# MLP gates in groups of four: modulation products in four row tiles, output turns as separate steps, gate and up weights in separate loads

## The chip, the cores and the metric

The kernel runs on one core of a Trainium2 chip. The metric is the device time of one execution in microseconds, as the median of several runs. The core's engines work side by side and each takes its instructions in the order written: TensorE (PE, matrix products, with the weight loads shown as PEld), VectorE (DVE), ScalarE (ACT), GpSimd (POOL) and SyncE (SP), which here issues nearly all DMA transfers. Data lie in SBUF, 128 partitions wide; products are written to PSUM, which has eight banks of 128 x 512 float32.

## What is computed

Eight sequences (NB = 8) of 512 steps and 512 features pass through a layer norm, and then through two branches whose product is added to the input:

```
xn = layernorm(x)
s  = mamba(xn)
g  = silu(ffn(xn))
out = x + s * g

mamba:  xz = xn @ W_in.T ; x_ssm, z = split(xz)
        x_conv = silu(causal_conv4(x_ssm) + conv_b)
        Bm, Cm, dt = x_conv @ W_x.T          (dt through softplus)
        h = exp(A*dt) * h + dt*Bm*x_conv     (scan over 512 steps, 1024 channels x 16 states)
        y = sum_states(h * Cm) + D * x_conv
        s = (y * silu(z)) @ out_W.T

ffn:    mod  = 0.1 * tanh(attention(rmsnorm(xn)) @ A)      (rank 16)
        h    = rmsnorm(xn)
        gate = silu(h @ W_in_base.T + (mod * (h @ A)) @ B)
        up   = h @ W_up_base.T
        ffn  = xn + (gate * up) @ W_down.T
```

The low-rank term `(mod * (h @ A)) @ B` is the modulation product: its contraction is only 16 deep, against 512 for `h @ W_in_base.T`. The MLP is 2048 wide, 16 blocks of 128 per batch.

## The kernel before

**Stages.** The first stage, some 800 us, does the norms and the attention of all batches and leaves the normalized inputs (`scr_x`), the modulation rows (`scr_m`) and the first batch's convolved input in HBM. The second stage, the rest, takes the eight batches one after the other. In each, the scan of batch b runs on DVE (L549 and L557), POOL (L551 and L562) and ACT (the decays, L537), and at the same time PE does the products of that batch's MLP (`gate_up`, `down_proj`), the z gates, the convolution inputs and step sizes of batch b+1 (`conv_in`, `step_size`) and the output projection of batch b-1 (`finish`).

**Order.** It is written out by a small planner. `batch_parts(b)` makes a list of parts, each with a number of units (one unit is one 128x512 product), its weight loads and a function. A batch has 64 scan steps of two chunks, 128 chunks in all. In every chunk the main loop first issues what earlier parts left for this chunk (the `(delay, function)` pairs that a part returns, delays counted in chunks), then as many parts as keep the units in step with the chunks, then a decay (ACT) and half a scan step (DVE). Every fourth step is followed by a burst of 8 small products that sums the states (`sum_states`, L574, into `y`). Weight loads are issued up to eight parts ahead, within a limit for each kind (`limits`).

**Banks.** Four PSUM banks serve all products in rotation, two from pool `ps_1` and two from `ps_2` (`bank`); the other four hold `y`, two decays and a copy of the scan's input factor. A part that asks for a bank waits until the work that used it four requests earlier has been read out.

**The gates.** `gate_up(b, fp)` handles two MLP blocks: two gate products of 4 units (`product(i, 0)`, L291), then `modulated`, which adds the modulation products to both banks (L300), two tanh on ACT (L306) and, one chunk later, two gates on DVE (`gate`, L312); then two up products (L291), each followed two chunks later by L317 on DVE. The modulation rows `modh` lie at partitions 0 to 15 and 32 to 47, and the low-rank weights `lob` likewise, so the two modulation products of a pair use two row tiles of PE.

```
for i in range(2):
    nc.tensor.matmul(
        st[i, 0], lhsT=lob[i * QD : i * QD + R, fp, :],
        rhs=modh[b][i * QD : i * QD + R, :], start=False, stop=True,
    )
```

**The weights.** `load_gu` (L218) loads a block's gate and up weights together, 512 KB, into one of three buffers, which is held until the up product is done.

**The output.** `finish(b, m)` projects one quarter of the output in two parts (L373). Its second part leaves behind: one chunk later `product` on DVE (L383) and the load of the input piece (L386), three chunks later `turn` (four transposes on PE, L392, into a bank of its own), five later `add` (DVE, L397), seven later `store` (L402). The buffers `f` are five in rotation: four hold what `down_proj` left, and the input pieces take them in turn.

**Convolution and z.** `conv_in` makes one product (L201) into a bank, then on ACT L259, three taps on DVE (L240), a tanh on ACT (L246) and a product on DVE (L250), after which the bank is free. `z_gate` makes a product (L201), a tanh (L277) and one DVE operation (L271). `finish_y` closes a block of `y` on DVE (L584, L585).

Of the kernel before, what the change touches and what calls it, by code (L numbers as in the profile page):

```python
# [39 lines left out]
def mamba_gated_ffn_kernel(  # L40
# [79 lines left out]
    lob = wp.tile([2 * QD, NF // 2, P], F32, tag="lob", name="lob")  # L120
# [8 lines left out]
    def constants():  # L129
        st = {}  # L130

        def loads():
            al = xcp.tile([P, 512], F32, tag="xc", name="al")
            st["al"] = al[:, : ND * NS].rearrange("p (d n) -> p d n", n=NS)
            nc.sync.dma_start(st["al"], a_log)
            for t, src in ((cw, conv_w), (cb, conv_b), (dsk, d_skip), (dtb, dt_bias), (wx, w_x)):
                nc.sync.dma_start(t, src)
            for i in range(2):
                nc.sync.dma_start(
                    lob[i * QD : i * QD + R],  # L140
                    lora_b.rearrange("r (f i c) -> i r f c", i=2, c=P)[i],
                )
# [140 lines left out]
    def gate_up(b, fp):  # L283
# [3 lines left out]
        def product(i, which):  # L287
            w = loaded["wgu", b, 2 * fp + i]
            ps = bank(f"ps_gu_{b}_{fp}_{i}_{which}")
            for kt in range(KT):  # L290
                nc.tensor.matmul(  # L291
                    ps, lhsT=w[:, which, kt, :], rhs=ht[b][:, kt, :],
                    start=(kt == 0), stop=(which == 1 and kt == KT - 1),
                )
            st[i, which] = ps
            return []

        def modulated():
            for i in range(2):
                nc.tensor.matmul(  # L300
                    st[i, 0], lhsT=lob[i * QD : i * QD + R, fp, :],
                    rhs=modh[b][i * QD : i * QD + R, :], start=False, stop=True,
                )
            for i in range(2):
                th = tmp.tile([P, S], F32, tag="th", name=f"gth_{b}_{fp}_{i}", bufs=3)
                nc.scalar.activation(th, st[i, 0], AF.Tanh, scale=0.5)  # L306
                st["th", i] = th
            return [(1, lambda: gate(0)), (1, lambda: gate(1))]

        def gate(i):  # L310
            m = mp.tile([P, S], F32, tag="m", name=f"m_{b}_{2 * fp + i}")
            nc.vector.scalar_tensor_tensor(m, st["th", i], 1.0, st[i, 0], ALU.add, ALU.mult)  # L312
            mlp[b, 2 * fp + i] = m

        def up(i):
            m = mlp[b, 2 * fp + i]
            nc.vector.scalar_tensor_tensor(m, m, 0.5, st[i, 1], ALU.mult, ALU.mult)  # L317

        def second(i):
            product(i, 1)  # L320
            loaded.pop(("wgu", b, 2 * fp + i))
            return [(2, lambda: up(i))]

        return [
            (4, [("wgu", lambda: load_gu(b, 2 * fp))], lambda: product(0, 0)),
            (4, [("wgu", lambda: load_gu(b, 2 * fp + 1))], lambda: product(1, 0)),
            (1, [], modulated),
            (4, [], lambda: second(0)),
            (4, [], lambda: second(1)),
        ]  # L330
# [33 lines left out]
    def finish(b, m):  # L364
# [3 lines left out]
        def out_proj(q):  # L368
# [8 lines left out]
            if q == 1:  # L377
                return [(1, product), (3, turn), (5, add), (7, store)]
# [10 lines left out]
        def turn():  # L389
# [3 lines left out]
            st["pt"] = ps  # L393

# [6 lines left out]
        def store():  # L401
# [4 lines left out]
            (5, [("wout", lambda: load_out(b, m, 1))], lambda: out_proj(1)),  # L406
        ]
# [181 lines left out]
    def batch_parts(b):  # L589

        pairs = [gate_up(b, fp) for fp in range(NF // 2)]
        convs, sizes = [], ([], [], [], [], [])
        parts = list(pairs[0])
        if 0 < b < NB - 1:
            parts.insert(1, (0, [], lambda: load_xn(b + 1)))
        if b + 1 < NB:
# [24 lines left out]
        for p in parts:  # L621
            while z < ND and done >= total * (8 * z + 5) / STEPS:
# [11 lines left out]
    limits = {"win": 3, "wgu": 3, "wd": 4, "wout": 3}  # L634
# [13 lines left out]
    def run_part():  # L648
        prefetch()
        units, loads, fn = queue[state["run"]]  # L650
# [596 lines left out]
    banks["second"] = ctx.enter_context(tc.tile_pool(name="ps_2", bufs=2, space=PSUM))  # L1247
    ps_y = ctx.enter_context(tc.tile_pool(name="ps_y", bufs=1, space=PSUM))
# [52 lines left out]
    for m in range(KT):  # L1301
        queue.extend(finish(NB - 1, m))
# [65 lines left out]
```

## Time and profile before

| | |
|---|---|
| median of 3 runs | 3187.24 us (3186.13 to 3191.59) |
| profiled execution | 3184.08 us |
| its span, first to last instruction | 3182.3 us |
| mean granted TensorE clock | 0.995 of full speed |
| gate and up products, L291 | 2048 instructions, 916.0 us busy |
| modulation products, L300 | 256 instructions, 72.1 us busy |
| gates on DVE, L312 | 128, mean 0.675 us |
| weight loads, wgu (L218) | 128 of 512 KB |
| output turns, L392 | 128 transposes, 19.4 us busy |
| SP waiting for PE before a wgu load | 481.6 us in 47 waits |
| SP waiting for PE before a scan load (L529) | 402.2 us in 99 waits |

The profile is of one execution; its span is 1.8 us shorter than the time of that execution, and its time 3.2 us below the median. Busy time of an engine counts the time in which at least one of its instructions ran. In lists of groups the columns are line, engine, operation, tiles written and read, count, busy us, mean ns of one, and the idle time of the engine just before, with what ended it. A row of the timeline merges neighbouring instructions of one line: start us, length in us, engine, line, operation, tiles, count, and in brackets the engine's idle time before it and what ended it. Instructions on PE are pipelined: each is shown longer than the distance from its start to the next one's.

### The profile page before, as it was taken

Reading aid. Unit: us, or ns where it says so; the run is one execution under the profiler, and the core shown is the slowest. Engines: PE = TensorE matmul, PEld = TensorE weight load, DVE = VectorE, ACT = ScalarE, POOL = GpSimd, SP = SyncE. Lnnn points to the kernel's source line nnn. Section 1 sums busy time; section 2 is a strip of 40 time slices with the busy share of each in tenths; the row PEclk is TensorE's granted clock in tenths of the full one; section 3 lists DMA queues with packets and bytes.
Section 4 is the critical chain, followed back from the end, with each engine's and each line's share of the span. In section 5 each row is a group of like instructions: output and inputs, shape, how many; then the busy total and the mean of one; then the engine's idle time right before and its main releaser. Section 6 shows DMA issues by size and latency. Waiting matters only on the chain.

```text
span 3182.3 us, 34018 instructions
## 1 busy us (share of the span) xinstructions
PE 3104.2 (98%) x11740; PEld 1365.5 (43%) x11740; DVE 2604.4 (82%) x3362; ACT 1336.9 (42%) x2279; POOL 1905.7 (60%) x876
## 2 busy tenths in 40 slices
PE   7999999988999999999999999999999999999999
PEld 4555555544333444344344434434443344344333
DVE  6877878865898889878878888898889878888884
ACT  4555555543444334333433334334334333443331
POOL 3111111100688877777777777777777777778884
PEclk9999999998999999999999999999999999999999
DMA  3111111101778785877677677768686777777674
GB/s 114 43 44 45 44 44 44 54 30 58 202 197 200 189 221 171 206 212 199 182 186 210 193 195 205 201 181 210 183 220 176 200 208 198 187 186 211 182 195 112
DMA packets 276284, 504.53 MB, mean 159 GB/s; under 512 B 28016, under 2 KB 159600, under 8 KB 271504
## 3 DMA queue, kind: packets, MB, share of 16 engines
q1 hardware_dynamic: 274704, 493.71, 57.8%
q0 software_dynamic: 1408, 8.65, 0.7%
q8 instruction: 93, 1.52, 0.2%
q14 instruction: 79, 0.65, 0.1%
HBM read 460.00 MB, written 42.29 MB: 158 GB/s over the span
## 4 chain that ended last, share of the span: by engine, by line
PE 90%; DVE 5%; ACT 2%; issue 1%; POOL 1%; DMA 1%; POOLq 0%; SPq 0%; ACTq 0%; DVEq 0%
PE ps_gu L291 27%; PE ps_acc L344 13%; PE ps_in L201 12%; PE y L574 7%; PE ps_out L373 7%; PE ps_pt L994 4%; PE ps_k L948 4%; PE s L963 3%; PE ps_q L948 3%; PE o_ps L1008 2%; PE ps_gu L300 2%; PE ps_z L930 2%; DVE x L557 1%; ACT pt L1001 1%; DVE conv L240 1%
## 5 line engine op out<-in xcount | busy, mean ns | idle before, releaser
L562 POOL TENSOR_TENSOR x<-x,cc 128x1024 f32<-128x1024 f32 x512 | 1208.0, 2359 | 543.5 <-DVE x L557 538.7
L557 DVE TENSOR_TENSOR_SCAN x<-decay,x 128x512 f32<-128x512 f32 x1024 | 1208.5, 1209 | 93.4 <-POOL x L551 91.4
L537 ACT ACTIVATE decay<-dt,an 128x511 f32<-128x511 f32 x1024 | 692.7, 687 | 656.6 <-DVE x L557 656.4
L291 PE MATMUL ps_gu<-ht,wgu 128*128 128x512 f32 x2048 | 916.0, 597 | 2.5 <-DVE m L312 1.6
L551 POOL TENSOR_TENSOR x<-x,bb 128x1024 f32<-128x1024 f32 x256 | 604.6, 2362 | 4.9 <-DMA x<-scr_c 4.9
L291 PEld LDWEIGHTS ps_gu<-ht,wgu 128*128 128x128 f32 x2048 | 380.5, 190 | 518.4 <-issue 467.4
L344 PE MATMUL ps_acc<-m,wd 128*128 128x512 f32 x1024 | 453.7, 595 | 0.0
L201 PE MATMUL ps_in<-xnt,win 128*128 128x512 f32 x960 | 434.9, 597 | 0.0
L1046 POOL DMA_DIRECT2D scr_m<-mod_t x8 | 4.0, 499 | 602.8 <-DVE mod_t L1045 522.1
L549 DVE TENSOR_TENSOR x<-x,dtb_ps 128x1024 f32<-128x1024 f32 x256 | 306.4, 1197 | 40.5 <-DMA x<-scr_c 39.4
L344 PEld LDWEIGHTS ps_acc<-m,wd 128*128 128x128 f32 x1024 | 192.0, 190 | 250.5 <-issue 246.7
L201 PEld LDWEIGHTS ps_in<-xnt,win 128*128 128x128 f32 x960 | 178.7, 190 | 245.8 <-issue 228.4
L979 ACT ACTIVATE p<-s,mx 128x384 f32<-128x384 f32 (+3 forms) x512 | 236.7, 528 | 92.8 <-DVE mx L973 90.5
L574 PE MATMUL y<-x,sel 128*32 128x512 f32 x2048 | 258.8, 599 | 9.0 <-POOL x L562 9.0
L373 PE MATMUL ps_out<-xc,wout 128*128 128x512 f32 x512 | 228.2, 597 | 0.0
L973 DVE TENSOR_REDUCE mx<-s 128x2 f32<-128x256 f32 (+3 forms) x256 | 211.0, 824 | 8.8
L994 PE MATMUL ps_pt<-ident,p 128*128 128x128 f32 x1280 | 197.3, 286 | 20.0 <-ACT pt L1001 14.7
L994 PEld LDWEIGHTS ps_pt<-ident,p 128*128 128x128 f32 x1280 | 142.0, 143 | 114.6 <-issue 38.1
L240 DVE SCALAR_TENSOR_TENSOR conv<-ps_in,cw,conv 128x511 f32<-128x511 f32 x168 | 125.4, 747 | 45.0 <-ACT conv L259 41.0
L999 DVE COPY pt<-ps_pt 128x512 f32<-128x512 f32 x160 | 109.3, 685 | 57.0 <-PE ps_pt L994 51.5
L969 DVE TENSOR_TENSOR s<-s,mask 128x256 f32<-128x256 f32 x256 | 109.0, 426 | 51.6 <-PE s L963 41.4
L373 PEld LDWEIGHTS ps_out<-xc,wout 128*128 128x128 f32 x512 | 95.2, 191 | 121.4 <-issue 121.4
(189 smaller groups left out, 2344.4 us busy)
## 6 DMA issues: line engine op xcount, KB each, us to landing
x<-scr_c SPq DMA_DIRECT2D x512, 512.0 KB
wgu<-in_w_ffn SPq DMA_DIRECT2D x128, 512.0 KB
win<-in_w_in SPq DMA_DIRECT2D x128, 256.0 KB
wd<-in_w_ffn SPq DMA_DIRECT2D x128, 256.0 KB
scr_c<-xc SPq DMA_DIRECT2D x64, 256.0 KB
wout<-in_out_w SPq DMA_DIRECT2D x64, 256.0 KB
xt<-in_x SPq DMA_DIRECT2D x32, 256.0 KB
scr_x<-xnT SPq DMA_DIRECT2D x8, 1024.0 KB
```

The lines of the kernel that those rows point to most:

```text
L201: nc.tensor.matmul(ps, lhsT=w[:, kt, :], rhs=xnt[b][:, kt, :], start=(kt == 0), stop=(kt == KT - 1))
L291: nc.tensor.matmul(ps, lhsT=w[:, which, kt, :], rhs=ht[b][:, kt, :], start=(kt == 0), stop=(which == 1 and kt == KT - 1),)
L344: nc.tensor.matmul(st["acc"], lhsT=w[:, j, :], rhs=mlp[b, f], start=(f == 0), stop=(f == NF - 1))
L373: nc.tensor.matmul(st["ps"], lhsT=w[:, d % 4, :], rhs=xc[b, d], start=(d == 0), stop=(d == ND - 1),)
L537: nc.scalar.activation(decay[n][:, 1:], spread[b][2][:, 1:], AF.Exp, scale=an[:, g // 4, g % 4 : g % 4 + 1])
L549: nc.vector.tensor_tensor(t, t, dtb_ps.unsqueeze(1).to_broadcast([P, 2, S]), ALU.mult)
L551: nc.gpsimd.tensor_tensor(t, t, spread[b][0].unsqueeze(1).to_broadcast([P, 2, S]), ALU.mult)
L557: nc.vector.tensor_tensor_scan(t, decay[n], t, 0.0, ALU.mult, ALU.add)
L562: nc.gpsimd.tensor_tensor(t, t, spread[b][1].unsqueeze(1).to_broadcast([P, 2, S]), ALU.mult)
L574: nc.tensor.matmul(y[ts(j, QD), :], lhsT=sel[:, i0 + n, :], rhs=xs[k - 3 + j][:, n, :], start=(i0 + n == 0), stop=(i0 + n == 3),)
L979: nc.scalar.activation(pr[:, 2 * i + n, :], sc[i][:, n, :w], AF.Exp, bias=mx[i][:, n : n + 1])
L994: nc.tensor.transpose(ps[:, ts(h, P)], probs[b, hg, qt][:, h, ts(kt, P)], ident)
```

## The change

The gates come in groups of four. `gate_up(b, fq)` makes four gate products into the four banks. The last gate's product is cut: its first unit, then the four modulation products (rows at partitions 0, 32, 64 and 96, each into its own bank), then its other three units. After that come the tanh of gates 0 and 1 at once, and those of 2 and 3 and the four gates spread over the next four chunks. The four up products follow as parts of their own. In `batch_parts` the output projection stands after the first group, in groups two to four the gate and up products are parted by a convolution or a turn, and a part marked `glued` isn't parted from the one before it by a z gate. `turn` is a part of one unit after the next quarter's projection, and leaves `add` two and `store` four chunks behind. `load_gu` loads one of the two weights, 256 KB, into one of six buffers. `modh` and `lob` have four copies or quarters of rows in place of two. `bank` takes two banks from one pool and then two from the other.

```diff
-        pool = banks["second"] if banks["second"] and banks["n"] % 2 else ps_1
+        pool = banks["second"] if banks["second"] and banks["n"] % 4 // 2 else ps_1
...
-        modh[b] = act.tile([2 * QD, S], F32, tag="modh", name=f"modh_{b}", bufs=1)
-        for i in range(2):
+        modh[b] = act.tile([4 * QD, S], F32, tag="modh", name=f"modh_{b}", bufs=1)
+        for i in range(4):
             nc.sync.dma_start(modh[b][i * QD : i * QD + R, :], scr_m[b])
...
-    lob = wp.tile([2 * QD, NF // 2, P], F32, tag="lob", name="lob")
+    lob = wp.tile([4 * QD, NF // 4, P], F32, tag="lob", name="lob")
...
-    def load_gu(b, f):
-        w = wp.tile([P, 2, KT, P], F32, tag="wgu", name=f"wgu_{b}_{f}", bufs=3)
-        nc.sync.dma_start(w, w_ffn[f][:, :2])
-        loaded["wgu", b, f] = w
+    def load_gu(b, f, which):
+        w = wp.tile([P, KT, P], F32, tag="wgu", name=f"wgu_{b}_{f}_{which}", bufs=6)
+        nc.sync.dma_start(w, w_ffn[f][:, which])
+        loaded["wgu", b, f, which] = w
...
-    def gate_up(b, fp):
+    def gate_up(b, fq):
...
+        def product(i, which, kts):
+            if kts[0] == 0:
+                st[i, which] = bank(f"ps_gu_{b}_{fq}_{i}_{which}")
+            w = loaded["wgu", b, 4 * fq + i, which]
+            for kt in kts:
                 nc.tensor.matmul(
+                    st[i, which], lhsT=w[:, kt, :], rhs=ht[b][:, kt, :], start=(kt == 0),
+                    stop=(kt == KT - 1 and (which == 1 or i == 3)),
+                )
...
+        def last():
+            product(3, 0, range(1))
+            for i in range(4):
                 nc.tensor.matmul(
+                    st[i, 0], lhsT=lob[i * QD : i * QD + R, fq, :],
+                    rhs=modh[b][i * QD : i * QD + R, :], start=False, stop=(i < 3),
                 )
+            product(3, 0, range(1, KT))
+            tanh(0)
+            tanh(1)
+            return [
+                (1, lambda: gate(0)), (1, lambda: tanh(2)), (2, lambda: gate(1)),
+                (2, lambda: tanh(3)), (3, lambda: gate(2)), (4, lambda: gate(3)),
+            ]
...
+        def part(i, which, units, fn):
+            p = units, [("wgu", lambda: load_gu(b, 4 * fq + i, which))], fn
+
+            return p + ("glued",) if which == 0 and i > 0 else p
+
+        gates = [part(i, 0, 4, lambda i=i: product(i, 0, range(KT))) for i in range(3)]
+        gates.append(part(3, 0, 5, last))
+        return gates, [part(i, 1, 4, lambda i=i: second(i)) for i in range(4)]
...
             if q == 1:
-                return [(1, product), (3, turn), (5, add), (7, store)]
+                return [(1, product)]
...
             st["pt"] = ps
+            return [(2, add), (4, store)]
...
-        pairs = [gate_up(b, fp) for fp in range(NF // 2)]
...
+        quads = [gate_up(b, fq) for fq in range(NF // 4)]
...
         if b > 0:
-            for m in range(KT):
-                parts += finish(b - 1, m)
-        for i in range(1, NF // 2):
-            for _ in range(2 if i == 4 else 1):
-                if convs:
-                    parts += convs.pop(0)
-            parts += pairs[i]
+            done = [finish(b - 1, m) for m in range(KT)]
+            parts += done[0][0] + done[1][0] + [done[0][1]] + done[2][0] + [done[1][1]]
+            parts += convs[0] + done[3][0] + [done[2][1]] + convs[1]
+            turns = [done[3][1]]
+        else:
+            parts += convs[0] + convs[1]
+            turns = []
+        parts += quads[1][0] + turns + convs[2] + quads[1][1] + convs[3] + convs[4]
+        parts += quads[2][0] + convs[5] + quads[2][1] + convs[6]
+        parts += quads[3][0] + convs[7] + quads[3][1]
...
-            while z < ND and done >= total * (8 * z + 5) / STEPS:
+            while z < ND and done >= total * (8 * z + 5) / STEPS and not p[3:]:
...
-    limits = {"win": 3, "wgu": 3, "wd": 4, "wout": 3}
+    limits = {"win": 3, "wgu": 6, "wd": 4, "wout": 3}
...
-    for m in range(KT):
-        queue.extend(finish(NB - 1, m))
+    done = [finish(NB - 1, m) for m in range(KT)]
+    queue.extend(done[0][0] + done[1][0] + [done[0][1]] + done[2][0] + [done[1][1]])
+    queue.extend(done[3][0] + [done[2][1], done[3][1]])
```

More of the change, by code (lines that the diff above doesn't have):

```diff
@@ L137, in loads @@
                 nc.sync.dma_start(t, src)
-            for i in range(2):
+            for i in range(4):
                 nc.sync.dma_start(
                     lob[i * QD : i * QD + R],
-                    lora_b.rearrange("r (f i c) -> i r f c", i=2, c=P)[i],
+                    lora_b.rearrange("r (f i c) -> i r f c", i=4, c=P)[i],
                 )
@@ L281, in z_gate @@
         return [(4, [("win", lambda: load_win(b, ND + d))], run)]
-    def gate_up(b, fp):
+    def gate_up(b, fq):
         st = {}
[L287 to L290, printed above, removed]
+        def product(i, which, kts):
[3 more added lines that the diff above has]
+            for kt in kts:
@@ L291, in product @@
                 nc.tensor.matmul(
-                    ps, lhsT=w[:, which, kt, :], rhs=ht[b][:, kt, :],
-                    start=(kt == 0), stop=(which == 1 and kt == KT - 1),
-                )
-            st[i, which] = ps
+                    st[i, which], lhsT=w[:, kt, :], rhs=ht[b][:, kt, :], start=(kt == 0),
+                    stop=(kt == KT - 1 and (which == 1 or i == 3)),
+                )
+            if kts[-1] == KT - 1:
+                loaded.pop(("wgu", b, 4 * fq + i, which))
@@ L296, in product @@
             return []
-        def modulated():
-            for i in range(2):
+        def last():
+            product(3, 0, range(1))
+            for i in range(4):
                 nc.tensor.matmul(
-                    st[i, 0], lhsT=lob[i * QD : i * QD + R, fp, :],
-                    rhs=modh[b][i * QD : i * QD + R, :], start=False, stop=True,
-                )
[L304 to L308, printed above, removed]
+                    st[i, 0], lhsT=lob[i * QD : i * QD + R, fq, :],
+                    rhs=modh[b][i * QD : i * QD + R, :], start=False, stop=(i < 3),
+                )
+            product(3, 0, range(1, KT))
[5 more added lines that the diff above has]
+            ]
@@ L310, in gate, with tanh @@
+        def tanh(i):
+            th = tmp.tile([P, S], F32, tag="th", name=f"gth_{b}_{fq}_{i}", bufs=3)
+            nc.scalar.activation(th, st[i, 0], AF.Tanh, scale=0.5)
+            st["th", i] = th
         def gate(i):
-            m = mp.tile([P, S], F32, tag="m", name=f"m_{b}_{2 * fp + i}")
+            m = mp.tile([P, S], F32, tag="m", name=f"m_{b}_{4 * fq + i}")
             nc.vector.scalar_tensor_tensor(m, st["th", i], 1.0, st[i, 0], ALU.add, ALU.mult)
-            mlp[b, 2 * fp + i] = m
+            mlp[b, 4 * fq + i] = m
@@ L315, in up @@
         def up(i):
-            m = mlp[b, 2 * fp + i]
+            m = mlp[b, 4 * fq + i]
             nc.vector.scalar_tensor_tensor(m, m, 0.5, st[i, 1], ALU.mult, ALU.mult)
         def second(i):
-            product(i, 1)
-            loaded.pop(("wgu", b, 2 * fp + i))
+            product(i, 1, range(KT))
             return [(2, lambda: up(i))]
[L324 to L330, printed above, removed]
+        def part(i, which, units, fn):
+            p = units, [("wgu", lambda: load_gu(b, 4 * fq + i, which))], fn
+            return p + ("glued",) if which == 0 and i > 0 else p
@@ L405, in finish @@
             (4, [("wout", lambda: load_out(b, m, 0))], lambda: out_proj(0)),
-            (5, [("wout", lambda: load_out(b, m, 1))], lambda: out_proj(1)),
-        ]
+            (4, [("wout", lambda: load_out(b, m, 1))], lambda: out_proj(1)),
+        ], (1, [], turn)
     def step_size(b):
@@ L589, in batch_parts @@
     def batch_parts(b):
-        pairs = [gate_up(b, fp) for fp in range(NF // 2)]
-        convs, sizes = [], ([], [], [], [], [])
-        parts = list(pairs[0])
+        quads = [gate_up(b, fq) for fq in range(NF // 4)]
+        sizes = ([], [], [], [], [])
+        parts = quads[0][0] + quads[0][1]
         if 0 < b < NB - 1:
             parts.insert(1, (0, [], lambda: load_xn(b + 1)))
+        convs = [[]] * ND
         if b + 1 < NB:
@@ L649, in run_part @@
         prefetch()
-        units, loads, fn = queue[state["run"]]
+        units, loads, fn = queue[state["run"]][:3]
         state["run"] += 1
@@ L1247, in mamba_gated_ffn_kernel @@
     banks["second"] = ctx.enter_context(tc.tile_pool(name="ps_2", bufs=2, space=PSUM))
+    banks["n"] = 1
     ps_y = ctx.enter_context(tc.tile_pool(name="ps_y", bufs=1, space=PSUM))
```

## The prediction

> **What bounds the kernel now.** First the busy shares, then the shares of the chain that ended last. TensorE (PE) works 98% of the span and carries 90% of the chain; VectorE (DVE) is next.
>
> ```profile
> PE 3104.2 (98%) x11740; PEld 1365.5 (43%) x11740; DVE 2604.4 (82%) x3362; ACT 1336.9 (42%) x2279; POOL 1905.7 (60%) x876
> ...
> PE 90%; DVE 5%; ACT 2%; issue 1%; POOL 1%; DMA 1%; POOLq 0%; SPq 0%; ACTq 0%; DVEq 0%
> ```
>
> An average over stages is not enough, so third the busy time by stretches: the first batch of the scan stage, a batch in the middle, the last one. Columns: PE, weight loads, DVE, ACT, POOL, then the granted clock and the DMA share.
>
> ```profile
> 805.00:1076.00 271.00, 264.65 (x794) 104.09 (x792) 243.23 (x262) 113.52 (x179) 219.28 (x94) 1.00 0.78 200
> 1430.00:1730.00 300.00, 300.00 (x912) 121.51 (x911) 255.68 (x278) 115.33 (x182) 224.71 (x97) 1.00 0.74 197
> 2883.00:3140.00 257.00, 255.44 (x786) 102.51 (x784) 217.07 (x224) 97.80 (x151) 215.89 (x94) 1.00 0.71 188
> ```
>
> The middle batches are PE from end to end: 300.00 of 300.00 us, and the list of waits has no PE entry between 1130 and 2630 us. DVE (85%), POOL (75%) and the DMA engines (74%) have room there. So in these batches PE time removed is time gained, as long as no PE wait takes its place. The first batch idles 6 us of 271, mostly for POOL ("y L574 <- POOL x L562", 5.7 us): there the scan side also counts.
>
> Fourth, the pieces of work that the change touches, in the timeline of PE (start, length, line, tiles, count). A 128x512 float32 product shows as two instructions.
>
> ```profile
> 1975.41 7.03 PE L291 MATMUL ps_gu<-ht,wgu 128*128 128x512 f32 x16
> 1982.37 1.92 PE L574 MATMUL y<-x,sel 128*32 128x512 f32 x16
> 1984.22 1.13 PE L300 MATMUL ps_gu<-modh,lob 16*128 16x512 f32 x4
> 1985.28 4.99 PE L291 MATMUL ps_gu<-ht,wgu 128*128 128x512 f32 x11
> ...
> 2998.10 3.70 PE L201 MATMUL ps_in<-xnt,win 128*128 128x512 f32 x8
> 3001.73 1.13 PE L300 MATMUL ps_gu<-modh,lob 16*128 16x512 f32 x4
> 3002.78 10.57 PE L291 MATMUL ps_gu<-ht,wgu 128*128 128x512 f32 x24
> 3013.28 1.92 PE L574 MATMUL y<-x,sel 128*32 128x512 f32 x16
> ```
>
> From start to start, 16 full instructions take 6.96 us: 0.429 each, and 0.093 more where the shape changes. Between 2998.10 and 3013.28 lie 32 full instructions and one modulation pair: 15.18 - 32 x 0.429 - 0.20 (the changes from and to the y bursts, there anyway) = 1.25 us for a pair between full products. It is 1.06 from start to start plus 0.20 for changing shape twice. The pair at 1984.22 follows a y burst, whose change of shape is paid anyway; it costs 1.06. So few columns of work cost so much because four instructions do what one product of two instructions would: two run side by side, twice.
>
> **The change part by part.**
>
> *Four row tiles at once.* Counted in that timeline, 52 of the 64 pairs stand between full products and 12 behind another change of shape: 52 x 1.255 + 12 x 1.057 = 77.9 us. The change runs 32 quads of eight instructions, each after the first product of the fourth gate and before its other three, so each pays two shape changes. A quad in four row tiles and four banks is in the trace already, in the attention scores:
>
> ```profile
> 313.67 1.14 PE L963 MATMUL s<-k,q 32*128 32x512 f32 x8
> 314.75 0.66 PE L994 MATMUL ps_pt<-ident,p 128*128 128x128 f32 x4
> ```
>
> Eight instructions in 1.08 us from start to start (1.07 in every such group I looked at; the four of a pass start 7 ns apart). So a quad costs 1.07 + 0.20 = 1.27, 32 of them 40.6, and the ideal gain is 37.3 us: 4.8 in a middle batch (8 pairs for 9.8, 4 quads for 5.1). The Trainium skill ("TensorE: Matmul & The Clock Gate", Measured speedup vs the span model) gives four row tiles 3.07 times the speed of one; by it a quad would take 4 x 0.858 / 3.07 = 1.12 instead of the row's 1.07, 1.5 us less gain in all. The row decides.
>
> *Four gates in four banks.* This is the new risk. PE has four rotating banks; before, gates held two, and the next product always had another. Now the product after a quad needs the bank of the quad's first gate, which is free when DVE has run its L312. From the quad's first start to the next product PE has 1.07 + 6 x 0.429 + 0.1 = 3.74 us of its own work. The tanh starts 1.16 us after a pair's start where ACT is free and lasts 0.59, the gate 0.675: 2.48 at best, and that is what the best pairs show. But DVE is a queue. The worst case of a middle batch, pair at 1490.50, DVE timeline:
>
> ```profile
> 1484.55 2.32 DVE L240 SCALAR_TENSOR_TENSOR conv<-ps_in,cw,conv 128x511 f32<-128x511 f32 x3 [2.73 <-ACT conv L259]
> ...
> 1489.63 4.55 DVE L557 TENSOR_TENSOR_SCAN x<-decay,x 128x512 f32<-128x512 f32 x4
> 1494.11 1.19 DVE L549 TENSOR_TENSOR x<-x,dtb_ps 128x1024 f32<-128x1024 f32 x1
> 1495.22 1.27 DVE L312 SCALAR_TENSOR_TENSOR m<-gth,ps_gu 128x512 f32<-128x512 f32 x2
> ```
>
> The first gate ends at 1495.89, 5.39 us after the pair began, because a convolution put 2.3 us in front. Over all 64 pairs it ends after 3.9 us at the median; the excess over 3.74 sums to 48.7 us, 24 us for half as many quads. That is one bound; the other is nothing. Between them I place DVE's work by hand from the changed program's order. Quad 1 (first of a batch): DVE is anchored on the end of a y burst 4.2 us before the quad, then y and gate products 1.43, two scans 2.4, one product 1.2: it waits for the tanh, gate at 2.5, no stall. Quad 3: two convolutions ahead, but 13 us of PE work lie between; done at 2.8. Quad 4: done at 2.5, and a y burst follows, which needs no bank. Quad 2 is the tight one: two convolutions and an output product ahead; from the first convolution 24 us before the quad DVE has no free time until the first gate, at 3.1 to 4.2: a stall of 0 to 0.5. I take 0.5 for six middle batches, 3.0 us. Gates two to four come one per chunk (a chunk is 300/128 = 2.34 us) while PE asks for a bank every 3.4 us: cover 0.5 to 5 us. What stands behind the waiting gate on DVE is a scan, and POOL's L562 behind it; both regain it, DVE having 15% free.
>
> The Trainium skill ("TensorEngine Tiling (Array Packing)", PSUM Bottleneck) speaks against the change: tiling speeds up TensorE, not the emptying of its banks, which can become the limit. If every quad met the worst row above, it would be right: 32 x (5.39 - 3.74) = 52.8 us, more than the gain.
>
> *Turns as own parts.* The same 128 transposes. DVE f L383 held them up 1.9 us in all, 1.6 of it in the last batch; a turn now stands behind the next output product, so this goes: gain 1.6. The store leaves after the turn as before. The load of the next input piece (L386) now waits on SP for the preceding turn to free its buffer; the scan's loads queue behind it, up to one output part (3.4 us). They run four steps (9.4 us) ahead, which hides it; uncovered it would be 3.4 x 2 x 7 = 48 us on DVE, of which its free 15% takes most.
>
> *Weights apart.* 256 loads of 256 KB for 128 of 512 KB, and 16 more 32 KB loads of the modulation rows, 18 a batch on a queue that issues some 144. The bytes stay. DMA is 74% busy and PE waited 0.9 us for a weight in the whole run. SP's waits get better if anything: the largest is L218 for PE, 481.6 us, a whole tile held until its second half is used. I take 0; bounds -2 and +2.
>
> *First and last batch.* The first has 4.8 us less PE work but waits for POOL already, so I take half, 2.4 (from 0 to 11.2, all of it and the idle 6.4). The last keeps 4.8: DVE has 40 us free there. The final wait for POOL (2.7 us) stays.
>
> **Sum.** 6 x 4.8 = 28.6; less 3.0; plus 2.4, 4.8 and 1.6: 34.4 us off. The profiled execution took 3184.08 (span 3182.3 and 1.8 around it), so 3149.7; the median of the runs shown is 3187.24, 3.2 above it, and on that footing 3152.8: **3153 us**, 1.1% faster.
>
> **Rivals.** (a) *The gates are late as in today's pairs*, 24 us of stalls instead of 3: gain 13, 3174. For it: the median of 3.9. Against: the hand schedule of the four positions, where PE work now lies between convolution and quad. (b) *The four tiles do not run together* because the fourth shares its bank with a running product: a quad costs as much as two pairs in a row, 2.11 + 0.20; 32 x 2.31 = 74, gain 4 and the turns' 1.6, 3182. Against: the score rows. (c) *Slower*: DVE's queue delays the first gate of every quad as in the latest pair of a middle batch, 52.8 us of stalls at the product after each quad against 37.4 gained: 3203. It decides from a mean stall of 37.4 / 32 = 1.17 us on, a gate ending 4.9 us after the quad's start. For it: three of the eight pairs in a middle batch already end at 5.0 to 5.4. Against: those follow a convolution's product by 7 us, the quads by 13 or more.
>
> **Chances and range.** A measurement of this kernel can tell about 0.2%, 6.4 us, from no change. My forecast 0.73, (a) 0.09, (b) 0.06, (c) 0.12. (b) lies just at the bound and counts as same. Faster 0.82, same 0.06, slower 0.12. The range goes down to 3143 (no stall, half of what the first batch could still give and a DMA gain: 34.4 + 3 + 4.4 + 2) and up to 3178, past (a).
>
> **What would show it.** The modulation line should have 256 instructions in 32 groups of eight, about 1.07 us from start to start, and some 38 us busy instead of 72.1. A middle batch should last about 294.5 us instead of 299.3 (from the first pair of one, at 1385.5, to that of the next, at 1684.8), PE still without idle time but for some half microseconds behind the second quad, named DVE m. Rival (a) or (c) would show as PE waiting for DVE's gate line 32 times; (b) as groups of 2.1 us. I am wrong if the middle batches have PE waits of more than a few us each, on banks, weights or POOL.

## The result, and the profile after

The changed kernel takes 3173.44 us (median of 6 runs, 3171.51 to 3179.3), the kernel before 3186.94 (6 runs, 3183.72 to 3191.59): a ratio of 0.996 with a 95% interval of 0.9948 to 0.9973. It is 13.5 us faster, inside the range, but 40% of the 34 us forecast. The number is rival (a)'s, 3174. That proves nothing for its mechanism, as will be seen: the gates were not late.

The changed kernel's busy shares, the shares of its chain, two groups of its PE list, and three stretches (two middle batches and the last one; columns as in the prediction):

```profile
PE 3081.8 (97%) x11740; PEld 1359.9 (43%) x11740; DVE 2605.3 (82%) x3362; ACT 1342.6 (42%) x2279; POOL 1904.8 (60%) x876
...
PE 80%; DVE 11%; POOL 4%; ACT 2%; issue 2%; DMA 2%; SPq 0%; POOLq 0%; ACTq 0%; DVEq 0%
```

```profile
L586 PE MATMUL y<-x,sel 128*32 128x512 f32 x2048 | 269.8, 601 | 11.9 <-POOL x L574 11.2
...
L304 PE MATMUL ps_gu<-modh,lob 16*128 16x512 f32 x256 | 36.5, 640 | 0.0
```

```profile
1130.00:1430.00 300.00, 298.65 (x920) 121.75 (x919) 256.52 (x279) 116.65 (x183) 224.18 (x97) 1.00 0.75 198
1430.00:1730.00 300.00, 296.87 (x911) 120.46 (x910) 255.40 (x277) 115.96 (x182) 224.00 (x96) 1.00 0.76 197
2883.00:3140.00 257.00, 254.33 (x797) 101.93 (x797) 217.03 (x224) 97.58 (x150) 214.81 (x93) 0.99 0.70 182
```

PE works 22.4 us less in all, and the modulation line went from 72.1 us busy to 36.5. But PE's share of the chain fell from 90% to 80%, while DVE's rose from 5% to 11% and POOL's from 1% to 4%. A middle batch, which had PE busy for all of its 300 us, now has 296.87. The line of the y bursts, L586 (L574 before), is busy 11.0 us longer with the same 2048 instructions (258.8 before). PE's list of waits from 1130 to 2630 us was empty before. Now it reads (line and tile, what it waited for: us in all, times, longest):

```profile
PE ps_gu L293 <- DMA wgu<-in_w_ffn: 4.1, 5, 1.2
PE ps_acc L355 <- DVE f L368: 3.3, 2, 1.6
PE y L586 <- POOL x L574: 1.3, 6, 0.4
```

These are the three kinds that the prediction named as its failure: weights, banks and POOL. The list alone sums to 8.7 us, 1.7 a batch, and so not the "more than a few us each" that it asked for; the rest of the loss hides in bursts that count as busy, as shown below.

The two profiled executions differ by 10.3 us, the medians by 13.5. To set the loss beside the forecast, the span is cut at the first down product (L344, now L355) of each batch. Each stretch between two cuts holds the gates of one batch:

| stretch | forecast, us | measured, us |
|---|---|---|
| up to the first cut (gates of the first batch) | -2.4 | +1.2 |
| six stretches (gates of the middle batches) | -25.6 | -7.7 |
| the seventh (gates of the last batch, two turns) | -6.4 | -4.0 |
| the rest | 0 | +0.3 |
| sum | -34.4 | -10.2 of a span 10.3 shorter |

Of the first row, 2.1 us had arisen by the start of the scan stage, in the run's first 62 us, where the change adds only two more loads of `lob`. There PE's granted clock was lower in this one execution: 0.86 from 50 to 62 us, against 1.00 before. The middle batches hold the loss. One by one, these stretches last 307.4, 297.8, 299.8, 297.6, 299.1 and 297.5 us after, against 309.8 and five times 299.4 to 299.7 before: every second batch gains next to nothing.

The quad is not the cause. PE's timeline of one quad in the changed kernel:

```profile
1688.60 1.45 PE L293 MATMUL ps_gu<-ht,wgu 128*128 128x512 f32 x3
1689.98 1.14 PE L304 MATMUL ps_gu<-modh,lob 16*128 16x512 f32 x8
1691.06 1.12 PE L293 MATMUL ps_gu<-ht,wgu 128*128 128x512 f32 x2
```

Eight instructions in 1.08 us from start to start, as in the score rows. The first gate, read from DVE's timeline, ends 2.48, 2.75, 2.48 and 3.27 us after the start of quads 1 to 4 of a middle batch; the cover is 3.74. No bank of a gate stalls PE in those batches. The three waits come from elsewhere.

**POOL, and through it the output bursts.** A y burst of 16 instructions takes 1.85 us to the next start. Twice a batch it now breaks in two. PE, then POOL, in the changed kernel:

```profile
2110.89 1.06 PE L586 MATMUL y<-x,sel 128*32 128x512 f32 x6
2112.11 1.90 PE L586 MATMUL y<-x,sel 128*32 128x512 f32 x10 [0.17 <-POOL x L574]
2113.95 0.70 PE L293 MATMUL ps_gu<-ht,wgu 128*128 128x512 f32 x1
```

```profile
2101.71 2.37 POOL L574 TENSOR_TENSOR x<-x,cc 128x1024 f32<-128x1024 f32 x1
2109.70 2.36 POOL L574 TENSOR_TENSOR x<-x,cc 128x1024 f32<-128x1024 f32 x1 [5.62 <-DVE x L569]
```

The burst lasts 3.06 us instead of 1.85, though the list of waits counts only 0.17 us of idle time: by the starts in the trace, a whole burst is four rounds of four instructions, 0.43 us apart, and this one is six rounds, of 3, 3, 4, 4, 1 and 1, which all count as busy. POOL's last product came late because POOL itself had waited 5.62 us for a scan. Why, DVE's timeline tells:

```profile
2102.18 2.31 DVE L240 SCALAR_TENSOR_TENSOR conv<-ps_in,cw,conv 128x511 f32<-128x511 f32 x3
2104.41 1.21 DVE L569 TENSOR_TENSOR_SCAN x<-decay,x 128x512 f32<-128x512 f32 x1
2105.54 0.66 DVE L250 SCALAR_TENSOR_TENSOR xc<-ps_in,conv 128x512 f32<-128x512 f32 x1
2106.12 2.31 DVE L240 SCALAR_TENSOR_TENSOR conv<-ps_in,cw,conv 128x511 f32<-128x511 f32 x3
2108.34 1.21 DVE L569 TENSOR_TENSOR_SCAN x<-decay,x 128x512 f32<-128x512 f32 x1
```

No gap: each row starts as the one before ends. Two convolutions stand between the scans, because the order puts convolutions 3 and 4 side by side. But the kernel before does this too, once a batch, and POOL waits just as long there (POOL, then PE, in the kernel before):

```profile
1512.56 2.35 POOL L562 TENSOR_TENSOR x<-x,cc 128x1024 f32<-128x1024 f32 x1 [5.62 <-DVE x L557]
1514.41 2.46 PE L574 MATMUL y<-x,sel 128*32 128x512 f32 x16
```

There the burst starts 1.85 us after POOL's last product does and takes 2.39 us; in the changed kernel it starts after 1.19 us and takes 3.06. So at this place DVE and POOL are no later than they were: PE is earlier, and the slack is used up. The other burst that now breaks, some 20 us earlier in the batch, took its 1.85 us before. All time inside bursts, from the first start of each to its last start, is 23.85 us a batch after, 21.9 before, 21.3 without any wait.

**Weights.** The first gate of a batch waits for its weight. PE, then SP's queue, in the changed kernel:

```profile
1368.59 7.13 PE L355 MATMUL ps_acc<-m,wd 128*128 128x512 f32 x16
1376.79 1.53 PE L293 MATMUL ps_gu<-ht,wgu 128*128 128x512 f32 x3 [1.06 <-DMA wgu<-in_w_ffn]
```

```profile
1355.68 0.37 SPq L223 DMA_DIRECT2D wd<-in_w_ffn  x1
1356.14 13.72 SPq L541 DMA_DIRECT2D x<-scr_c  x4
1369.91 3.41 SPq L218 DMA_DIRECT2D wgu<-in_w_ffn  x6
```

The parts of the next batch join the list only when that batch begins. Then four scan loads stand ahead on SP, which wait for a y burst to free their buffers, and the weight is issued 5.8 us before PE could use it. From start to start this costs 0.98 us a batch on average from 1130 to 2630 us; the list of waits has 4.1 us for the five. The kernel before had the same order on SP, and no wait. SP, then PE, at the end of the same batch before:

```profile
1357.22 10.29 SPq L529 DMA_DIRECT2D x<-scr_c  x4
1367.56 1.05 SPq L218 DMA_DIRECT2D wgu<-in_w_ffn  x2
1376.64 7.03 PE L291 MATMUL ps_gu<-ht,wgu 128*128 128x512 f32 x16
```

There the weight had 9.1 us, as a z product of eight instructions and 16 down instructions followed the burst that frees the buffers; now only the 16 do.

**A bank.** In batches 0, 2, 4 and 6 PE waits at the start of the fourth down product:

```profile
1649.85 3.60 PE L355 MATMUL ps_acc<-m,wd 128*128 128x512 f32 x8
1653.28 1.02 PE L445 MATMUL ps_bb<-parts_p,lift 128*128 128x512 f32 x2
1655.94 2.41 PE L355 MATMUL ps_acc<-m,wd 128*128 128x512 f32 x5 [1.64 <-DVE f L368]
```

The change takes two banks from one pool and then two from the other. A batch makes 65 requests, so its alignment moves by one from batch to batch. By the bank numbers in the built program of batch 2, the fourth down product gets the bank of the third, whose last reader (`f`, L368, on DVE) has not run yet; in batch 1 it gets that of `ps_dt`, and before the change it got that of `ps_cc`, both read long before. So the bank that a request gets is not always that of four requests earlier, as the text ahead of the prediction has it: `ps_cc` stands two requests ahead of this product.

Counted from start to start over the six stretches, and set against the kernel before: 11.0 us in bursts, 4.4 for weights (one wait of before, 1.1, taken off) and 3 x 1.8 for the bank, together 20.8. Missing between the 28.6 of PE work taken out of the middle batches and the 7.7 found are 20.9. That is an account, and the experiments test it.

### The profile page after: what moved, and what is told of

Read it like the earlier page. It is cut to its first block, busy times and chain, and to the rows that moved or that the text cites. A ratio compares the mean times of both kernels' runs of the same rounds, so it can differ in the third digit from the quotient of the medians.

```text
span 3172.0 us, 34348 instructions
## 1 busy us (share of the span) xinstructions
PE 3081.8 (97%) x11740; PEld 1359.9 (43%) x11740; DVE 2605.3 (82%) x3362; ACT 1342.6 (42%) x2279; POOL 1904.8 (60%) x876
## 4 chain that ended last, share of the span: by engine, by line
PE 80%; DVE 11%; POOL 4%; ACT 2%; issue 2%; DMA 2%; SPq 0%; POOLq 0%; ACTq 0%; DVEq 0%
PE ps_gu L293 22%; PE ps_acc L355 11%; PE ps_in L201 11%; PE ps_out L384 7%; PE y L586 7%; DVE x L569 4%; PE ps_pt L1010 4%; PE ps_k L964 4%; PE s L979 3%; PE ps_q L964 3%; PE o_ps L1024 2%; POOL x L574 2%; DVE conv L240 2%; PE ps_z L946 2%; POOL x L563 1%
## 5 line engine op out<-in xcount | busy, mean ns | idle before, releaser
L574 POOL TENSOR_TENSOR x<-x,cc 128x1024 f32<-128x1024 f32 x512 | 1207.8, 2359 | 532.5 <-DVE x L569 519.2
L355 PE MATMUL ps_acc<-m,wd 128*128 128x512 f32 x1024 | 455.5, 597 | 6.6 <-DVE f L368 6.6
L355 PEld LDWEIGHTS ps_acc<-m,wd 128*128 128x128 f32 x1024 | 190.6, 190 | 263.2 <-issue 250.0
L586 PE MATMUL y<-x,sel 128*32 128x512 f32 x2048 | 269.8, 601 | 11.9 <-POOL x L574 11.2
```

The costliest lines, as they stand in the source:

```text
L355: nc.tensor.matmul(st["acc"], lhsT=w[:, j, :], rhs=mlp[b, f], start=(f == 0), stop=(f == NF - 1))
L574: nc.gpsimd.tensor_tensor(t, t, spread[b][1].unsqueeze(1).to_broadcast([P, 2, S]), ALU.mult)
L586: nc.tensor.matmul(y[ts(j, QD), :], lhsT=sel[:, i0 + n, :], rhs=xs[k - 3 + j][:, n, :], start=(i0 + n == 0), stop=(i0 + n == 3),)
```

## Experiments

Ratios are to the kernel before, run on the same chip beside each experiment; where I compare with the changed kernel, it is by its median of 3173.44. The intervals are 4 to 8 us wide to each side, so a few us are read from the traces and not from the times alone. Lines of a kernel keep the numbers of the one that it starts from, but for a few added or left-out lines.

**The kernel before, without the modulation products.** What is the PE time of the pairs worth where the rest of the order stays?

```diff
...
-            for i in range(2):
-                nc.tensor.matmul(
-                    st[i, 0], lhsT=lob[i * QD : i * QD + R, fp, :],
-                    rhs=modh[b][i * QD : i * QD + R, :], start=False, stop=True,
-                )
```

> The kernel before with its 64 pairs of modulation products left out (the low-rank term is not computed). By the prediction's own measure they cost 77.9 us of PE time. Theory 'new waits' (PE time removed is time gained unless the order of the work puts a new wait in its place; the order before has its convolutions evenly spread): 60 to 78 us faster, a middle batch 290 to 291 us against 299.4. Rival 'floor' (DVE and POOL, with what they wait for, already need about 298 us for a middle batch, so PE time removed is not gained by any order): less than 20 us faster, y bursts waiting for POOL everywhere.

Measured: 3135.21, ratio 0.9832 (0.9808 to 0.9856), 51 us less for 77.9 us of PE work. It lies between the two theories: a middle batch lasts 292.65 us, 6.8 less for 9.8 taken out. PE, which never waited there, now waits for the gates (4.5 us in 1130 to 2630), and the bursts lengthen from 21.9 to 23.8 us a batch. So PE time converts at about two thirds even in the old order: "PE time removed is time gained" was too much before any edit of the order. The bursts lose as much here (23.8) as in the changed order (23.85). The expectation calls the old order's convolutions evenly spread; two of the eight stand side by side there too.

**The bank alone.** One request is skipped where the alignment is the bad one.

```diff
             if q == 0:
+                if m == 2 and banks["n"] % 2 == 0:
+                    banks["n"] += 1
                 st["acc"] = bank(f"ps_acc_{b}_{m}")
```

> The changed kernel, with one bank request skipped where needed so that down_proj's third and fourth accumulators never meet in one bank. Theory 'new waits': the wait of PE ps_acc L355 for DVE f L368 (1.64 us in every second batch, 6.6 us in the whole run) goes, and 4 to 7 us with it. Rival 'floor': the wait goes and comes back as a wait for POOL in the next y burst: under 1.5 us.

Measured: 3165.47, 0.9924 (0.9901 to 0.9947), 8.0 us below the changed kernel; four times 1.64 would be 6.6. The same place in its PE timeline:

```profile
1647.63 3.60 PE L357 MATMUL ps_acc<-m,wd 128*128 128x512 f32 x8
1651.07 1.02 PE L447 MATMUL ps_bb<-parts_p,lift 128*128 128x512 f32 x2
1651.93 2.31 PE L357 MATMUL ps_acc<-m,wd 128*128 128x512 f32 x5
```

The next product starts 0.86 us behind the small one's start instead of 2.66. The middle batches are all alike now, 297.2 to 297.8 us, with bursts (23.86) and weights (0.98) unchanged. The bank's part of the account is shown.

**The convolutions spread.** One convolution between any two groups instead of two side by side; the last goes into the down projection.

```diff
...
-        parts += quads[1][0] + turns + convs[2] + quads[1][1] + convs[3] + convs[4]
-        parts += quads[2][0] + convs[5] + quads[2][1] + convs[6]
-        parts += quads[3][0] + convs[7] + quads[3][1]
+        parts += quads[1][0] + turns + convs[1] + quads[1][1] + convs[2]
+        parts += quads[2][0] + convs[3] + quads[2][1] + convs[4]
+        parts += quads[3][0] + convs[5] + quads[3][1] + convs[6]
...
-                parts += down
+                parts += down[:1] + convs[7] + down[1:]
```

> The changed kernel with its convolutions spread: one after every four parts of gates or ups, the last in the first down product, none next to another. Theory 'new waits', with DVE locally overloaded where three convolutions and four ups come within 40 us: the waits of y bursts for POOL (1.9 us a middle batch) fall under 0.5 us a batch, 8 to 14 us faster than the changed kernel in all. Rival 'floor': DVE's total is the same, so no more than 3 us. Rival 'late burst' (the bursts stand too early for POOL's own latency wherever the convolutions are): no more than 3 us, the waits move to other bursts.

Measured: 3171.11, 0.9949 (0.993 to 0.9969): 2.3 us less, which these intervals can't tell from nothing, and a miss. Bursts fall to 22.35 us a batch, 1.5 of the 1.95 that the account gives them, and the middle batches to 296.6 to 298.7, but the first stretch lasts 309.3 again instead of 307.4 and the seventh 273.0 instead of 269.2. It shows that the place of the convolutions bears on how late POOL is for a burst; a place free of loss for all eight it did not find. PE also waits for gates again, 1.8 us from 1130 to 2630.

**The bursts one step later.** If only the burst's date is too early for the scan, moving it helps without touching DVE. It holds the scan's buffers longer, so there is one more of them and one weight buffer less.

```diff
...
-    limits = {"win": 3, "wgu": 6, "wd": 4, "wout": 3}
+    limits = {"win": 3, "wgu": 5, "wd": 4, "wout": 3}
...
-    scan = ctx.enter_context(tc.tile_pool(name="scan", bufs=10))
+    scan = ctx.enter_context(tc.tile_pool(name="scan", bufs=11))
...
-                bursts[k + 2] = k
+                bursts[k + 3] = k
```

> The changed kernel with each y burst one scan step later (issued three steps after its last step, not two), 11 scan buffers, and, to make room for them, 5 buffers for gate and up weights. Theory 'new waits': the waits of y bursts for POOL nearly go, 8 to 14 us faster than the changed kernel if the lost weight buffer costs nothing. Rival 'floor': the scan itself is late, so the burst waits just as long a step later, or the gates do: under 3 us.

Measured: 3169.05, 0.994 (0.9921 to 0.9958), 4.4 us less. Bursts take 21.31 us a batch, the value without any wait: this part of the account is shown. But the time came back elsewhere. PE's waits for weights rose from 5.0 to 13.3 us in the whole run, and those for gates in the first batch from 1.1 to 7.1. That the scan loads ahead of the weights now wait for a later burst is the likely reason for the first; the lost weight buffer is another, which this run can't tell apart. The expectation missed that bursts and weights are coupled.

**The weights' place in the queue.** The next batch's parts join the list eight steps before that batch begins, so that its first weights can be issued.

```diff
...
+            if s == STEPS - 8 and b + 1 < NB:
+                parts = batch_parts(b + 1)
+                coming = sum(p[0] for p in parts)
+                queue.extend(parts)
```

> The changed kernel with the next batch's parts put on the list eight scan steps before the batch begins, so that its first gate weights are issued ahead of scan loads that wait for a y burst. Theory 'new waits': PE's waits for wgu (5.0 us in seven waits) go, 4 to 6 us faster than the changed kernel, a middle batch down by 1.0 us. Rival 'queue': the earlier loads hold SP up and the scan loads come late instead: no gain, DVE waiting for x from HBM.

Measured: 3165.73, 0.9936 (0.9915 to 0.9956), 7.7 us less. SP's queue at the end of the same batch:

```profile
1363.37 1.45 SPq L218 DMA_DIRECT2D wgu<-in_w_ffn  x3
1364.91 0.53 SPq L541 DMA_DIRECT2D x<-scr_c  x1
1365.48 1.06 SPq L218 DMA_DIRECT2D wgu<-in_w_ffn  x2
```

Weights and scan loads alternate, and in the middle batches PE waits for no weight; the other two waits stand unchanged (3.3 for the bank, 1.3 for POOL). The weights' part is shown.

**The repairs together.** First spread convolutions, bank and queue; then late bursts, bank and queue; then all four.

> The changed kernel with three repairs at once: convolutions spread (as in the third run), one bank request skipped (as in the second), weights ahead. Theory 'new waits': the three waits are separate and their sizes add: a middle batch at 294.6 (the PE work alone) plus 0.3 to 1 us, so 295 to 295.6; the run 17 to 22 us faster than the changed kernel, 3152 to 3156. Rival 'floor': removing one wait feeds the next, a middle batch not under 296.5.

> The changed kernel with the y bursts a step later (11 scan buffers, 5 weight buffers), the bank request skipped and the weights ahead; the convolutions stay where the change put them. Theory 'new waits': y bursts at 1.85 us each, a middle batch at 294.6 to 295.2, the run 3150 to 3156. Rival 'floor': not under 296.5 a batch.

> All four repairs: spread convolutions, bank, weights ahead, late bursts. Theory 'new waits': no PE wait of size left in the middle batches, 294.6 us each, within 1 us of the better of the two runs before it. Rival 'floor': no better than 296.5.

| | median, us | ratio to before | a middle batch, us |
|---|---|---|---|
| spread, bank, queue | 3155.19 | 0.9902 (0.9882 to 0.9922) | 295.7 |
| late bursts, bank, queue | 3141.62 | 0.9856 (0.9839 to 0.9872) | 293.9 |
| all four | 3147.43 | 0.9879 (0.9859 to 0.9898) | 295.1 |

Late bursts, bank and queue make the best kernel of the study that does the whole computation, 1.4% faster than the kernel before. The edits gain 8.0, 7.7 and 4.4 us one by one and 31.8 together, in part for the reason seen above: late bursts cost weights until the queue is mended, also with five weight buffers. Its middle batches have no PE wait at all, as this window shows:

```profile
1300.00:1600.00 300.00, 300.00 (x925) 122.85 (x924) 258.77 (x280) 117.26 (x185) 230.01 (x100) 1.00 0.77 202
```

PE is busy for all 300 us again, with DVE no less busy than before. All four together are worse than three: PE waits for gates on DVE ten times, 3.9 us, from 1130 to 2630, where the kernel with three has no wait. The likely reason, not shown, is that the spread convolutions now stand before the gates on DVE, while the late bursts had already taken the other cost away.

**The first batch of the repaired kernel.** What is left of PE's waits in the best kernel, from 800 to 1130 us:

```profile
PE ps_in L201 <- DVE m L323: 7.9, 3, 4.0
PE ps_gu L293 <- DMA wgu<-in_w_ffn: 1.9, 1, 1.9
PE ps_gu L293 <- DVE m L323: 1.7, 1, 1.7
PE ps_gu L293 <- DVE mod_t L1063: 0.8, 1, 0.8
```

Here the wait that the prediction feared is seen: in the first batch the first gates of quads 2 to 4 end 5.8 to 7.8 us after the quad's start, and the next product waits for their bank. So the convolutions were spread in this batch alone.

```diff
...
+            convs = [[]] + convs
...
+        parts += quads[1][0] + turns + convs[2] + quads[1][1] + convs[3]
+        parts += (convs[4] if b else []) + quads[2][0] + (convs[5] if b else convs[4])
```

> The seventh run's kernel (late bursts, bank request skipped, weights ahead) with the convolutions spread in the first batch alone, where PE still waits 9.6 us for gates on DVE. Theory 'new waits': in the first batch, which has no output projection between the first and the second group, DVE is overloaded by convolutions next to the gates; spread, 4 to 8 us of these waits go, the run 3134 to 3139. Rival: the first batch is bound by the scan's total on DVE and POOL: no gain, 3141 to 3143.

Measured: 3141.39, 0.9852 (0.9826 to 0.9878), the same as without it. The gates' waits fell from 9.6 to 3.9 us, but PE now waits 2.2 us for ACT ahead of the small step-size product `ps_v`, and the second batch's first down product comes no earlier (at 1294.6 us against 1292.8): a miss. That the first batch is short of DVE and POOL time, and not of a better order of convolutions, is a guess.

**Late bursts in the kernel before.** Was the burst's date a loss that the kernel had all along? With its memory the later burst needs one scan load less ahead.

```diff
...
-                    load_scan(k + 4)
+                    load_scan(k + 3)
...
-                bursts[k + 2] = k
+                bursts[k + 3] = k
```

> The kernel before with y bursts a step later, and scan loads three steps ahead in place of four so that ten buffers suffice. Theory 'new waits': before has 0.6 us of y waits in a middle batch (21.9 us in bursts against 21.3 without waits), so 2 to 6 us faster; the seventh run's 44 us are then the change's PE saving with its waits repaired. Rival 'bursts': the late burst is worth tens of us in any order, and the quads little: more than 15 us faster.

Measured: 3224.85, 1.0116 (1.0085 to 1.0146), slower. The bursts are clean (21.31 us a batch), but the scan's loads come late: 86.8 us of DVE waiting for them between 1130 and 2630. It says nothing on the bursts, as two things changed in it; from the trace of before they could give at most 21.9 - 21.3 = 0.6 us in a middle batch. What it does show is that, with late bursts, the lack of the fourth load ahead costs some 38 us.

**The changed order without the quads.** Is there a floor under the changed kernel, the scan's, that no PE saving gets past? Both kernels lose the quads and nothing else, first the changed kernel, then the best one.

> The changed kernel with its 32 quads of modulation products left out (the low-rank term is not computed): 40.6 us less PE work by the prediction's measure. The share that shows in the time is the exchange rate of PE time in this order. Theory 'new waits': the order already has PE waiting for the scan, so half or less, 10 to 22 us faster than the changed kernel. Rival 'PE bound': 36 to 41 us.

> The seventh run's kernel (late bursts, bank request skipped, weights ahead) with its quads of modulation products left out: again 40.6 us less PE work. Theory 'new waits': here PE has no wait in the middle batches and the bursts have a step in hand, so most of it shows, 28 to 41 us, 3101 to 3114, a middle batch 289 to 290.5. Rival 'floor': DVE, at 87% there, and POOL hold a batch at 293: under 10 us.

The changed kernel: 3143.01, 0.987 (0.9855 to 0.9885), 30.4 us less for 40.6 us of PE work, a miss: no floor, three quarters convert. Its three waits stay at much the same size (weights 4.9, bank 3.3 and POOL 1.2 us in 1130 to 2630), which speaks for waits of the order and against a limit of DVE. Set beside the first experiment, both without modulation, the new order is 7.8 us slower than the old.

The best one: 3127.88, 0.9824 (0.9808 to 0.9841), only 13.7 us less, a miss to the other side. Its timeline shows a part of why, behind the fourth and the second group of gates of a batch:

```profile
1554.64 6.60 PE L293 MATMUL ps_gu<-ht,wgu 128*128 128x512 f32 x15
1561.93 3.27 PE L201 MATMUL ps_in<-xnt,win 128*128 128x512 f32 x7 [0.69 <-DVE m L318]
...
1467.70 2.31 PE L201 MATMUL ps_in<-xnt,win 128*128 128x512 f32 x5
1469.84 0.60 PE L400 MATMUL ps_turn<-ident,f 128*128 128x128 f32 x4
1471.29 3.27 PE L201 MATMUL ps_in<-xnt,win 128*128 128x512 f32 x7 [0.84 <-DVE m L318]
```

The quad is part of its own cover. Without its 1.27 us the product after the gates comes too early for the first gate's bank ten times, 4.5 us, in 1130 to 2630. Five times more, 4.2 us, the bank is that of the third gate: there a turn of four short transposes stands between, and the product behind it comes 0.5 us later instead of the 3.4 of a full one. So the cover of 3.74 us that the prediction worked out is real, with 0.5 us to spare in the tightest quad and 1.0 to 1.3 in the others. These waits take 1.7 us of the 5.1 taken out of a middle batch, which lasts 291.3 us, 2.6 less; up to the second batch's down products nothing is gained at all (1295.3 us against 1292.8). What takes the rest is not worked out. The Trainium skill ("TensorEngine Tiling (Array Packing)", PSUM Bottleneck) says that tiling speeds TensorE and not the emptying of its banks; the middle batches of the changed kernel show no wait of PE for a gate's bank. The waits here come in a run that has no modulation products in row tiles.

## Why the prediction was off by 21 us

**Right: what the quad costs.** 1.08 us from start to start, 36.5 us busy in all (38 forecast). The four tiles run together; rival (b) is out.

**Right in the main: the gates' banks.** No stall in the middle batches where 3 us were set aside. The hand schedule gave 2.5, 3.1 to 4.2, 2.8 and 2.5 us for the first gates and the trace has 2.48, 2.75, 2.48 and 3.27: the tight one is the fourth, not the second. So rivals (a) and (c) are out too, though (a)'s number came true: PE waits for no gate in any of those batches.

**Right: the last batch and the turns.** 4.0 us measured for 6.4, and the missing part is there by name: this stretch has a bank wait of 1.6 and a weight wait of 0.5. The turns' waits fell from 1.9 to 0.3 us.

**Wrong: "PE time removed is time gained, as long as no PE wait takes its place", resting on "DVE having 15% free".** This is the step that failed: 25.6 us forecast for the middle batches, 7.7 found. The sum set 3.0 us aside for waits at gates and nothing for those that came, at bursts, weights and a bank. The first half of the step was already too much, since in the old order the removal of the pairs converts by two thirds. The second took an average for a local fact. DVE is 85% busy over a batch and has no gap in the 17 us or so around two convolutions side by side. There scans are late, then POOL. That was so before, too; with less PE work the burst comes sooner and meets it, and a second burst is now late as well: 1.95 us a batch. I had traced DVE's queue by hand up to the gates, and not to the scans that wait behind them.

**Wrong: weights apart at nothing, bounds -2 and +2.** 5.0 us of PE waits in the whole run. I counted bytes and issues; what mattered was the order on SP, where a weight stands behind scan loads that wait for PE. The forecast that SP's waits get better held for the weights themselves (L218 for PE, 187.2 us instead of 481.6), not for the scan loads (527.3 instead of 402.2). The scan loads stood ahead of the first weight before the change as well, with 9.1 us to spare for the weight instead of 5.8. That the parting of the loads is what brought this about was not tested: a changed kernel with joint loads was not tried. Shown is that the place in the queue decides.

**Wrong: the order of the banks, not costed at all.** The line stands in the diff, and no term of the sum belongs to it. It cost 4 x 1.64 = 6.6 us of idle time, 4 x 1.8 from start to start, by the run 8.0. The old alternation under the new order was not tried.

**Unsettled: the first batch.** A gain of 2.4 forecast; 0.9 measured if the 2.1 us lost before it are taken out. Its repair gave nothing, and its waits are mixed (POOL, gates, one weight); the cause stays open.

With the three waits repaired, a middle batch is 293.9 us, below the forecast 294.5 by about the 0.6 that the kernel before lost in bursts, and the run is 44 us faster than before. So the arithmetic of the saving was right; what it lacked was a price for what less PE work and the new order do at three places. How much of the 44 us the repairs would have given to the kernel before was not settled.

## What to carry to other kernels

When an engine is busy without a gap, its saved time is only a ceiling: ask of each other queue how many us later it could deliver before this engine waits, at the crowded place and not on the average. An edit that only reorders (which bank comes next, in what order loads are issued) gets a term of its own, found by following the rotation through several batches, because a count that is odd shows its fault only in every second one. If waits of several kinds appear together, repair them together before judging any: one by one these gave 20 us, together 32.

## What the runs showed that was not expected

A wait inside a burst of column-tiled products (four side by side, each into its own 32 rows of y) costs several times its idle time: 0.17 us shown, 1.2 us lost, because the products behind it run in six rounds instead of four. Look at a burst's length from start to start, not only at the list of waits.

Also a wait can cost the clock. In the best kernel PE waited 1.91 us for a weight in the first batch, and then eight instructions took 5.21 us from start to start instead of 3.43; windows of 6 us around it show the granted clock, and the last one stands behind another wait of 1.91 us, for a gate at 860.91:

```profile
806.00:812.00 6.00, 6.00 (x20) 1.99 (x18) 4.13 (x4) 2.70 (x5) 2.36 (x1) 1.00 1.03 238
812.00:818.00 6.00, 4.09 (x7) 1.69 (x7) 5.36 (x7) 1.91 (x4) 3.44 (x2) 0.76 1.05 337
818.00:824.00 6.00, 6.00 (x15) 2.77 (x14) 2.43 (x4) 1.24 (x3) 3.58 (x2) 0.96 1.04 266
861.00:867.00 6.00, 6.00 (x14) 2.67 (x15) 6.00 (x7) 3.02 (x5) 5.20 (x4) 1.00 0.89 201
```

The clock column falls from 1.00 to 0.76, so the first wait cost twice its length; behind the second, as long, it stayed at 1.00. So the length alone doesn't decide. Full products behind PE waits in the scan stages of all these traces ran at full speed after each wait under 1.9 us (among them those of 1.06 and 1.64 us shown above), at either speed after waits of 1.9 to 3.1 us, and partly at half speed after each of the six waits over 3.1 us.
